# Masked attention over gathered neighbours on one core: all operations placed by a list schedule made at build time, the weighting split by slots over two engines

## The chip, the core and the metric

The kernel runs on one core of a Trainium2 chip. A core has five engines with a queue each: TensorE (PE in the profile; PEld is its weight loads) for matmuls, VectorE (DVE), ScalarE (ACT), GpSimd (POOL) and SyncE (SP), which here only issues DMAs. Engines run side by side, take their own instructions in order, and wait for each other by semaphores. Data lies in SBUF (128 partitions), in PSUM, where matmuls write, and in DRAM. The metric is the device time of one launch in microseconds, the median of several runs.

## The reference

One layer of attention on a graph of 1024 nodes, for 16 batches of 1024 x 512 inputs and 8 heads of 64. The adjacency matrix is sparse, and all batches share it:

```
h = maximum(layernorm(x), 0)
q, k, v = h @ Wq + bq, h @ Wk + bk, h @ Wv + bv        # each (16, 1024, 8 heads, 64)
scores  = einsum('bihd,bjhd->bhij', q, k) / sqrt(64) + where(adj == 0, -1e9, 0)
x       = x + einsum('bhij,bjhd->bihd', softmax(scores), v)
```

## The kernel before

The kernel never forms the 1024 x 1024 scores. It sorts the nodes by their number of neighbours (lines 124 to 155), so that a tile of 128 rows holds rows with lists of about equal length, and makes for every row the list of its neighbours (`list_of`, `longest`, `pieces`, lines 245 to 310). Tile 7 has the shortest lists, 2 entries, tile 0 the longest, 12; what the longest rows have beyond 12 goes into extra "list rows", pieces of 4 entries that stand as a tile of their own, number -1. All this is done once, and the batches begin behind it.

For each batch and each of its 8 tiles: `load_x` gathers 128 rows of x by an indirect DMA; `stats` takes mean and variance and GpSimd the power -1/2 (line 182); `norm` normalises on ScalarE; `flip` transposes on PE and copies back on ScalarE; `proj_kv` projects k and v (line 204, eight PE instructions for one projection); `store_kv` adds the bias on VectorE and stores both to DRAM through SP (lines 219 and 221).

The attention of a batch goes in 14 units (`UNITS`, lines 44 to 59), each of 2 to 4 slots of one tile's lists; 8 of the 14 have 4 slots. A slot is one neighbour for each of 128 rows. For unit i: `gather` fetches k and v rows of its slots, one indirect DMA of 512 KB for each slot, issued by GpSimd (line 348) into one of five buffers g; `multiply` (line 358) multiplies k by the queries and `score` (line 363) sums by heads, both on VectorE; ScalarE takes the exponent (line 365) and weighs v, one instruction for each slot and head (line 372). For units 10 to 12 VectorE weighs all of v instead (`BY_VECTOR`, line 378). `weigh` also folds units of 4 slots to 2 on VectorE (line 380), except in the last batch; `add_up` adds the slots in PSUM by matmuls with the identity, or for the list rows with the matrix that hands them to their owners (line 393). `finish` scales by the sum of the weights (lines 404 to 417), and GpSimd adds x (line 422) and stores the rows by an indirect DMA (line 423).

The order on PE, VectorE, ScalarE and GpSimd is written out by hand: lines 480 to 527 loop over the units. In step i stand `gather(i + 3)`, then `weigh(i - 1)`, then `multiply(i)` and `score(i)` with up to two halves of the next batch's projections between them (`HALVES`: how many in each step), then `add_up(i - 1)`, the next tile's queries and the last tile's `finish`. The projections run one batch ahead of the attention, and x is loaded three tiles ahead of them. Only SP's queue isn't ordered by hand.

Of the kernel before, what the change touches and what calls it, by code (L numbers as in the profile page):

```python
# [14 lines left out]

# [46 lines left out]
BY_VECTOR = (10, 11, 12)  # L62


def main_path(tc, x, adj, Wq, bq, Wk, bk, Wv, bv, out, sums, cover):
# [4 lines left out]
    NT = N // P  # L70
    DC = D // P
    NU = len(UNITS)
# [4 lines left out]
    with ExitStack() as ctx:  # L77
        pool = lambda name, bufs=1, **k: ctx.enter_context(tc.tile_pool(name=name, bufs=bufs, **k))
        const = pool("const")
        xpool = pool("xpool", 16)  # L80
        hpool = pool("hpool", 2)
        htpool = pool("htpool", 13)
        kvpool = pool("kvpool", 3)
        gpool = pool("gpool", 5)
        work = pool("work", 2)
        small = pool("small", 4)
        dram = pool("dram", 3, space=bass.MemoryType.DRAM)
        psum = bass.MemoryType.PSUM
        ps_h = pool("ps_h", 1, space=psum)
        ps_kv = pool("ps_kv", 2, space=psum)  # L90
        ps_q = pool("ps_q", 2, space=psum)
        ps_a = pool("ps_a", 2, space=psum)
# [65 lines left out]
        X, HN, HT, KV, ST = {}, {}, {}, {}, {}  # L158
# [4 lines left out]

        def nth(b, t):
            return b * NT + NT - 1 - t
# [8 lines left out]
        def stats(n):  # L174
            b, t = tile_at(n)
            st = small.tile([P, nc.vector.BN_STATS_DIM], F32, tag="st", name=f"st_{b}_{t}")
            mv = small.tile([P, nc.vector.BN_AGGR_DIM], F32, tag="mv", name=f"mv_{b}_{t}")
            rstd = small.tile([P, 1], F32, tag="rstd", name=f"rstd_{b}_{t}")
            nc.vector.bn_stats(st, X[n])  # L179
            nc.vector.bn_aggr(mv, st)  # L180
            nc.vector.tensor_scalar_add(rstd, mv[:, 1:2], EPS)  # L181
            nc.gpsimd.tensor_tensor(rstd, rstd, minus_half, ALU.pow)  # L182
            ST[n] = mv, rstd

        def norm(n):
            b, t = tile_at(n)
            mv, rstd = ST.pop(n)
            shift = small.tile([P, 1], F32, tag="shift", name=f"shift_{b}_{t}")
            nc.vector.scalar_tensor_tensor(shift, mv[:, 0:1], -1.0, rstd, op0=ALU.mult, op1=ALU.mult)  # L189
            HN[n] = hpool.tile([P, D], F32, tag="h", name=f"h_{b}_{t}")  # L190
            nc.scalar.activation(HN[n], X[n], AF.Relu, bias=shift, scale=rstd)  # L191

        def flip(n):
            b, t = tile_at(n)
            hn = HN.pop(n)
            pt = ps_h.tile([P, DC, P], F32, tag="pht", name=f"pht_{b}_{t}")
            for c in range(DC):
                nc.tensor.transpose(pt[:, c, :], hn[:, ts(c, P)], ident)  # L198
            HT[n] = htpool.tile([P, DC, P], F32, tag="hT", name=f"hT_{b}_{t}")
            nc.scalar.copy(HT[n], pt)  # L200
# [4 lines left out]

        KVT, PT = {}, {}
# [6 lines left out]
        def store_kv(n, j):  # L213
# [3 lines left out]
            if j == 0:  # L217
                KVT[n] = kvpool.tile([P, 2, D], F32, tag="kvt", name=f"kvt_{b}_{t}")
            nc.vector.tensor_tensor(KVT[n][:, j, :], PT.pop((n, j)), bias["kv"[j]], ALU.add)  # L219
            if j == 1:  # L220
                nc.sync.dma_start(KV[b][ts(t, P), :], KVT.pop(n).rearrange("p j d -> p (j d)"))
# [44 lines left out]
        def pieces():  # L266
# [3 lines left out]
            flag = small.tile([P, PIECES], F32, tag="flag", name="flag")  # L270
            count = small.tile([P, 1], F32, tag="count", name="count")
# [7 lines left out]
            end = small.tile([P, 1], F32, tag="end", name="end")  # L279
# [10 lines left out]
            part = small.tile([P, 1], F32, tag="part", name="part")  # L290
            nc.vector.tensor_tensor(part, place[:, 0:1], p_list[:, width - 1 : width], ALU.subtract)
            pick = small.tile([P, PIECES], F32, tag="pick", name="pick")
            nc.vector.tensor_scalar(pick, iota[:, :PIECES], part, None, op0=ALU.is_equal)
            picked = small.tile([P, PIECES, PIECE], F32, tag="picked", name="picked")
# [9 lines left out]
            at = small.tile([P, SLOTS], F32, tag="at", name="at")  # L304
# [3 lines left out]
            used = small.tile([P, SLOTS], F32, tag="used", name="used")  # L308
# [4 lines left out]
        Q, PQ, G, ACC = {}, {}, {}, {}  # L313
# [3 lines left out]
        tiles = B * NT  # L317
        total = B * NU

# [9 lines left out]
        def queries(b, t):  # L329
            pt = PQ[b, t] = ps_q.tile([P, D], F32, tag="q", name=f"pq_{b}_{t}")  # L330
            if t >= 0:
                project(pt, "q", nth(b, t))
                HT.pop(nth(b, t))
            else:
                nc.tensor.matmul(pt, owner, Q[b, 0], start=True, stop=True)

        def add_bias(b, t):
            pt = Q[b, t] = PQ.pop((b, t))
            if t == 0:
                Q[b, t] = work.tile([P, D], F32, tag="q0", name=f"q0_{b}")  # L340
            if t >= 0:
                nc.vector.tensor_tensor(Q[b, t], pt, bias["q"], ALU.add)

        def gather(i):
            b, t, w, c, count = unit(i)
            G[i] = gpool.tile([P, UMAX, 2, D], F32, tag="g", name=f"g_{b}_{i % NU}")
            for s in range(count):
                nc.gpsimd.indirect_dma_start(  # L348
                    out=G[i][:, s].rearrange("p j d -> p (j d)"),
                    out_offset=None,  # L350
                    in_=KV[b][:],
                    in_offset=on(ap=index[:, c + s : c + s + 1], axis=0),
                )
# [6 lines left out]
        def score(i):  # L360
# [4 lines left out]
            nc.scalar.activation(weights[:, w, :], sc, AF.Exp, scale=HD**-0.5)  # L365
# [350 lines left out]
```

## Time and profile before

| | |
|---|---|
| time, median of 3 runs (lowest to highest) | 2898.34 us (2897.23 to 2902.49) |
| the profiled execution's own time | 2899.34 us |
| its span, first to last instruction | 2897.6 us |
| mean granted TensorE clock | 0.874 |
| mean rate over the span | 190 GB/s |
| first gather issued / first multiply | 156.2 / 163.6 us |

The page gives for each engine the busy time and its share of the span. A group of instructions is named by line, engine, operation and tiles, `out<-in`, followed by its count, its busy time and mean length, and by the idle time of its engine just before such instructions with what ended it. The view of waits sums those idle times by who waited for whom. The timeline gives start and length in us from the start of the span. Lengths within a queue can overlap a little, since an instruction starts while the one before it writes its last results.

### The profile page before, as it was taken

How to read it: one execution, taken by the hardware profiler on the slowest of the kernel's cores; microseconds unless marked ns; L12 is line 12 of the kernel's file. 1: busy time of each engine (PE TensorE's matmuls, PEld its weight loads, DVE VectorE, ACT ScalarE, POOL GpSimd, SP SyncE). 2: the span in 40 equal slices, each digit the busy share in tenths (PEclk: the TensorE clock that was granted, in tenths of full speed). 3: DMA queues.
4: the chain of work that ended last, by engine and by line, in shares of the span. 5: the costliest groups of instructions: out<-in, count | busy, mean ns of one | idle time of the engine just before them, and what ended most of it. 6: DMA issues, size and time to landing. Idle time of an engine off the chain costs nothing.

```text
span 2897.6 us, 20683 instructions
## 1 busy us (share of the span) xinstructions
PE 2125.6 (73%) x4727; PEld 915.5 (32%) x4727; DVE 1772.4 (61%) x2426; ACT 1339.5 (46%) x5142; POOL 1345.2 (46%) x1298
## 2 busy tenths in 40 slices
PE   3777776877867777776867777687777867777675
PEld 1333332333323333332323333233333323333221
DVE  6744664657566575665747566474755647566675
ACT  1143364453635535364453535535363453535573
POOL 2144444454545455444544444544544445454552
PEclk9898898988988888888988988888888988988897
DMA  5155546565555556556565655556555555555673
GB/s 196 62 200 170 194 169 213 180 215 186 196 178 196 198 196 208 191 167 218 188 215 178 210 171 188 208 195 211 188 181 197 189 207 184 204 178 181 237 242 117
DMA packets 153953, 550.66 MB, mean 190 GB/s; under 512 B 18784, under 2 KB 18784, under 8 KB 153824
## 3 DMA queue, kind: packets, MB, share of 16 engines
q0 software_dynamic: 132224, 474.02, 48.4%
q1 hardware_dynamic: 21600, 75.24, 6.6%
q8 instruction: 41, 0.67, 0.1%
q14 instruction: 88, 0.72, 0.1%
HBM read 448.53 MB, written 100.66 MB: 190 GB/s over the span
## 4 chain that ended last, share of the span: by engine, by line
DVE 22%; issue 22%; ACT 21%; POOL 17%; DMA 11%; PE 7%; POOLq 0%; DVEq 0%; SPq 0%; ACTq 0%
ACT g L372 20%; POOL g L348 11%; DMA x<-in_x_dram,perm 10%; DVE scores L363 7%; DVE g L358 3%; PE acc L393 3%; DVE g L380 3%; DVE kvt L219 2%; POOL o L422 2%; DVE st L179 2%; POOL out_dram L423 2%; PE pv L204 2%; PE pk L204 1%; DMA g<-kv,index 1%; DVE g L378 1%
## 5 line engine op out<-in xcount | busy, mean ns | idle before, releaser
L372 ACT ACTIVATE g<-g,weights 128x64 f32<-128x64 f32 x4608 | 1119.9, 333 | 11.4 <-issue 3.6
L348 POOL DMA_INDIRECT g<-kv,index x768 | 776.5, 1011 | 415.7 <-issue 218.7
L393 PE MATMUL acc<-g,ident 128*128 128x512 f32 x988 | 574.9, 711 | 391.1 <-DVE g L380 245.8
L365 ACT ACTIVATE weights<-scores 128x32 f32<-128x32 f32 (+2 forms) x224 | 43.0, 192 | 1138.2 <-DVE scores L364 1129.7
L204 PE MATMUL pk<-wk,hT 128*128 128x512 f32 x1024 | 529.5, 666 | 0.0
L422 POOL TENSOR_TENSOR o<-o,x 128x512 f32<-128x512 f32 x128 | 164.3, 1284 | 708.3 <-DVE o L417 707.0
L204 PE MATMUL pq<-wq,hT 128*128 128x512 f32 x1024 | 473.6, 606 | 0.0
L204 PE MATMUL pv<-wv,hT 128*128 128x512 f32 x1024 | 468.8, 601 | 0.0
L380 DVE TENSOR_TENSOR g<-g 128x1024 f32<-128x1024 f32 x120 | 147.0, 1225 | 496.9 <-ACT g L372 495.4
L363 DVE TENSOR_REDUCE scores<-g 128x32 f32<-128x2048 f32 (+2 forms) x224 | 444.0, 1982 | 5.9 <-ACT weights L365 2.8
L393 PEld LDWEIGHTS acc<-g,ident 128*128 128x128 f32 x988 | 204.2, 219 | 701.6 <-issue 326.5
L198 PE MATMUL pht<-ident,h 128*128 128x128 f32 x512 | 101.3, 330 | 326.2 <-ACT h L191 319.9
L179 DVE BATCH_NORM_STATS2 st<-x 128x6 f32<-128x512 f32 x128 | 88.3, 690 | 345.9 <-DMA x<-in_x_dram,perm 313.4
L358 DVE TENSOR_TENSOR g<-g,pq 128x2048 f32<-128x2048 f32 (+2 forms) x160 | 296.9, 1856 | 4.7 <-DMA g<-kv,index 4.0
L204 PEld LDWEIGHTS pk<-wk,hT 128*128 128x128 f32 x1024 | 214.3, 221 | 227.5 <-issue 227.5
L204 PEld LDWEIGHTS pq<-wq,hT 128*128 128x128 f32 x1024 | 202.1, 198 | 260.6 <-issue 259.6
L204 PEld LDWEIGHTS pv<-wv,hT 128*128 128x128 f32 x1024 | 199.7, 195 | 256.9 <-issue 254.0
L182 POOL TENSOR_TENSOR rstd<-rstd,minus_half 128x1 f32<-128x1 f32 x128 | 132.3, 1034 | 303.9 <-DVE rstd L181 297.6
L191 ACT ACTIVATE h<-x,shift,rstd 128x512 f32<-128x512 f32 x128 | 103.8, 811 | 290.6 <-DVE shift L189 279.7
L198 PEld LDWEIGHTS pht<-ident,h 128*128 128x128 f32 x512 | 65.0, 163 | 435.2 <-ACT h L191 426.5
L170 POOL DMA_INDIRECT x<-in_x_dram,perm x128 | 129.9, 1015 | 71.5 <-DVE perm L155 39.3
L423 POOL DMA_INDIRECT out_dram<-o,perm x128 | 132.3, 1033 | 36.3 <-POOL o L422 33.5
(138 smaller groups left out, 1090.6 us busy)
## 6 DMA issues: line engine op xcount, KB each, us to landing
kv<-kvt SPq DMA_DIRECT2D x128, 512.0 KB, 2.6
g<-kv,index POOLq DMA_INDIRECT x768
adj<-in_adj_dram SPq DMA_DIRECT2D x8, 512.0 KB, 8.0
x<-in_x_dram,perm POOLq DMA_INDIRECT x128
out_dram<-o,perm POOLq DMA_INDIRECT x128
wk<-in_L_gnn_Wk_dram SPq DMA_DIRECT2D x1, 1024.0 KB
wv<-in_L_gnn_Wv_dram SPq DMA_DIRECT2D x1, 1024.0 KB
wq<-in_L_gnn_Wq_dram SPq DMA_DIRECT2D x1, 1024.0 KB
```

The source lines that it names most:

```text
L179: nc.vector.bn_stats(st, X[n])
L182: nc.gpsimd.tensor_tensor(rstd, rstd, minus_half, ALU.pow)
L198: nc.tensor.transpose(pt[:, c, :], hn[:, ts(c, P)], ident)
L204: nc.tensor.matmul(pt, HT[n][:, c, :], W[name][:, c, :], start=(c == 0), stop=(c == DC - 1))
L348: nc.gpsimd.indirect_dma_start(out=G[i][:, s].rearrange("p j d -> p (j d)"), out_offset=None, in_=KV[b][:], in_offset=on(ap=index[:, c + s ...
L358: nc.vector.tensor_tensor(k, k, Q[b, t][:, None, :].to_broadcast([P, count, D]), ALU.mult)
L363: nc.vector.tensor_reduce(sc, heads(G[i][:, :count, 0, :]), AX.X, ALU.add)
L372: nc.scalar.activation(v[:, s, h, :], v[:, s, h, :], AF.Identity, scale=weights[:, c + s, h : h + 1])
L380: nc.vector.tensor_tensor(v[:, 0:2], v[:, 0:2], v[:, 2:4], ALU.add)
L393: nc.tensor.matmul(ACC[b, home], owner_t if t < 0 else ident, v[:, s, :], start=(u == units[0] and s == 0), stop=(u == units[-1] and s == ...
L422: nc.gpsimd.tensor_tensor(o, o, X.pop(nth(b, t)), ALU.add)
L423: nc.gpsimd.indirect_dma_start(out=out_rows, out_offset=on(ap=perm[:, t : t + 1], axis=0), in_=o[:], in_offset=None, element_offset=b * N * D)
```

## The change

A planner (`Plan`, `plan_of`) replaces the order written out by hand. It lists every operation with its engine, a length, a place (the unit in which it is wanted), what it comes after and which buffers it uses. It then walks through time: an engine that is free takes the operation with the lowest place that has all it needs and a buffer. The order in which operations were taken is the order in which they are written, so each engine's queue is fixed when the program is built.

Four things change in the work itself. The last slot of every unit (`BY_VECTOR = {2: 1, 3: 1, 4: 1}`) is weighted by VectorE, with an exponent of its own, and the others by ScalarE; before, VectorE did all slots of units 10 to 12 and none of the others. A unit of 4 slots is folded twice, to 2 and to 1, so that PE adds one slot for it. The power -1/2, its variance and its shift are taken for pairs of tiles. And the queries of tile 0 stay in PSUM, with a copy by ScalarE for the list rows' query. Pools for small tiles are larger (8 instead of 4); the number of big buffers is the same.

```diff
-BY_VECTOR = (10, 11, 12)
+BY_VECTOR = {2: 1, 3: 1, 4: 1}
+POOLS = dict(x=16, h=2, pht=1, hT=13, pkv=2, kvt=3, q=2, q0=1, g=5, acc=2, o=2)
+class Plan:
+    def add(self, key, engine, length, place, after=(), uses=(), delay=0.15, moves=0.0):
+        self.number[key] = len(self.ops)
+        self.ops.append((key, engine, length, place, after, uses, delay, moves))
+    def ordered(self, bufs):
...
+        while True:
+            for e in engines:
+                if free[e] > now:
+                    continue
+                passed = []
+                while ready[e]:
+                    place, i = heapq.heappop(ready[e])
+                    key, _, length, _, _, uses, delay, moves = ops[i]
+                    if can_start(ops[i]):
...
+                        result.append(key)
+                        free[e] = end = now + length
...
+def plan_of(B):
...
+    for n in range(tiles):
+        b, j = divmod(n, NT)
+        p = (b - 1) * NU + j * rate
+        add(("load_x", n), "POOL", 1.25, p - 7, uses=[("x", n)], delay=4.5, moves=0.75)
+        add(("stats", n), "DVE", 0.9, p - 5, [("load_x", n)], [("x", n)])
+        if n % 2:
+            add(("variance", n // 2), "DVE", 0.16, p - 5, [("stats", n - 1), ("stats", n)])
+            add(("power", n // 2), "POOL", 0.6, p - 4.4, [("variance", n // 2)])
+            add(("shift", n // 2), "DVE", 0.16, p - 4.4, [("power", n // 2)])
...
+        for s, slot in enumerate(slots):
+            add(slot, "POOL", 1.25, i - 4 + 0.1 * s, stored, [g], delay=4.0, moves=1.5)
+        vector = BY_VECTOR[count]
+        add(("multiply", i), "DVE", 0.15 + 0.533 * count, i, slots + [q_of[q]], [g, q])
+        add(("score", i), "DVE", 0.35 + 0.533 * count, i + 0.01, [("multiply", i)], [g])
+        add(("exponent", i), "ACT", 0.4, i + 0.1, [("score", i)])
+        weighed = [("weigh_v", i)]
+        add(("weigh_v", i), "DVE", 0.15 + 0.533 * vector, i + 0.6, [("exponent", i)], [g])
+        for s in range(count - vector):
+            weighed.append(("weigh_s", i, s))
+            add(("weigh_s", i, s), "ACT", 1.97, i + 0.5 + 0.1 * s, [("exponent", i)], [g])
+        if folds(b, B, count):
+            add(("fold", i, 2), "DVE", 1.22, i + 1.3, weighed, [g])
+            add(("fold", i, 1), "DVE", 0.69, i + 1.35, [("fold", i, 2)], [g])
+            weighed = [("fold", i, 1)]
...
+def folds(b, B, count):
+    return count == 4 and b < B - 1
...
+        def exponent(i):
+            b, t, w, c, count = unit(i)
+            nc.scalar.activation(weights[:, w, :], scores[:, w, :], AF.Exp, scale=HD**-0.5)
+            own = scores[:, c + count - BY_VECTOR[count] : c + count, :]
+            nc.scalar.activation(own, own, AF.Exp, scale=HD**-0.5)
+        def weigh_v(i):
+            b, t, w, c, count = unit(i)
+            n = BY_VECTOR[count]
+            v = heads(G[i][:, count - n : count, 1, :])
+            own = scores[:, c + count - n : c + count, :, None]
+            nc.vector.tensor_tensor(v, v, own.to_broadcast([P, n, H, HD]), ALU.mult)
+        def fold(i, n):
+            v = G[i][:, :, 1, :]
+            nc.vector.tensor_tensor(v[:, 0:n], v[:, 0:n], v[:, n : 2 * n], ALU.add)
...
-            count = 2 if count == 4 and b < B - 1 else count
+            count = 1 if folds(b, B, count) else count
...
-        for n in range(min(3, tiles)):
-            load_x(n)
-        with tc.manual_schedule(engines={mybir.EngineType.PE, mybir.EngineType.DVE, mybir.EngineType.Activation, mybir.EngineType.Pool}):
...
+        with tc.manual_schedule(engines=set(engines)):
+            for name, *args in plan_of(B):
+                do[name](*args)
```

Three places show the order. In the rows a tile's name is followed by batch and unit (`g_8_9` is the buffer of batch 8, unit 9) or by batch and tile (`pk_9_1`), and then by the number of its buffer. First VectorE in batch 8, before, from the reduction of unit 9 to the multiply of unit 10:

```order
L363 TENSOR_REDUCE scores_205<-g_8_9_7923 128x32
L364 TENSOR_TENSOR scores_205<-scores_205,mask_201 128x32
L342 TENSOR_TENSOR q0_8_8184<-pq_8_0_8141,bq_rows_135 128x512
L404 TENSOR_REDUCE sums_58<-weights_206 128x8
L413 TENSOR_SCALAR sums_58<-sums_58 128x8
L415 RECIPROCAL inv_8_2_8188<-sums_58 128x8
L417 TENSOR_TENSOR o_8_2_8190<-acc_8_2_8003,inv_8_2_8188 128x512
L380 TENSOR_TENSOR g_8_9_7923<-g_8_9_7923 128x2x512
L179 BN_STATS st_10_5_8200<-x_10_5_8127 128x6
L180 BN_AGGR mv_10_5_8201<-st_10_5_8200 128x2
L181 TENSOR_SCALAR rstd_10_5_8202<-mv_10_5_8201 128x1
L358 TENSOR_TENSOR g_8_10_7971<-g_8_10_7971,q0_8_8184 128x4x512
```

And in the changed kernel, from the mask of unit 10 to its first fold:

```order
L551 TENSOR_TENSOR scores_211<-scores_211,mask_207 128x32
L574 TENSOR_TENSOR g_8_9_7690<-g_8_9_7690 128x2x512
L405 TENSOR_TENSOR kvt_9_1_7938<-pk_9_1_7913,bk_rows_133 128x512
L574 TENSOR_TENSOR g_8_9_7690<-g_8_9_7690 128x512
L564 TENSOR_TENSOR g_8_10_7785<-g_8_10_7785,scores_211 128x512
L545 TENSOR_TENSOR g_8_11_7811<-g_8_11_7811,pq_8_-1_7908 128x4x512
L372 SCALAR_TENSOR_TENSOR shift_40_7969<-mv_40_7740,rstd_40_7775 128x2
L405 TENSOR_TENSOR kvt_9_1_7938<-pv_9_1_7940,bv_rows_137 128x512
L550 TENSOR_REDUCE scores_211<-g_8_11_7811 128x32
L551 TENSOR_TENSOR scores_211<-scores_211,mask_207 128x32
L615 TENSOR_TENSOR o_8_1_7988<-acc_8_1_7936,inv_8_1_7888 128x512
L574 TENSOR_TENSOR g_8_10_7785<-g_8_10_7785 128x2x512
```

Before, a unit's fold (L380) stood between its own reduction and the next unit's multiply. Now the fold of unit 9 (L574, `128x2x512`) stands behind the reduction of unit 10, and that of unit 10 behind the reduction of unit 11; the second fold (`128x512`) follows one instruction later, and the weighting of the last slot (L564) stands behind the previous unit's folds.

Second PE at the same place of the program. Before, from the queries of tile 0 to the accumulation of unit 10:

```order
L204 MATMUL pq_8_0_8141<-wq_133,hT_8_0_7135 128x512 x4
L393 MATMUL acc_8_1_8146<-g_8_8_7880,ident_111 128x512 x2
L198 MATMUL pht_10_6_8207<-ident_111,h_10_6_8139 128x128 x4
L204 MATMUL pk_10_7_8214<-wk_125,hT_10_7_8074 128x512 x4
L204 MATMUL pv_10_7_8225<-wv_129,hT_10_7_8074 128x512 x4
L393 MATMUL acc_8_1_8146<-g_8_9_7923,ident_111 128x512 x2
L335 MATMUL pq_8_-1_8242<-q0_8_8184,owner_202 128x512
L198 MATMUL pht_10_5_8256<-ident_111,h_10_5_8238 128x128 x4
L204 MATMUL pk_10_6_8263<-wk_125,hT_10_6_8212 128x512 x4
L204 MATMUL pv_10_6_8273<-wv_129,hT_10_6_8212 128x512 x4
L393 MATMUL acc_8_0_8288<-g_8_10_7971,ident_111 128x512 x2
```

And now:

```order
L394 MATMUL pq_8_0_7851<-wq_139,hT_8_0_7062 128x512 x4
L589 MATMUL acc_8_2_7781<-g_8_7_7573,ident_117 128x512 x3
L385 MATMUL pht_9_0_7901<-ident_117,h_9_0_7787 128x128 x4
L522 MATMUL pq_8_-1_7908<-q0_8_7891,owner_208 128x512
L394 MATMUL pk_9_1_7913<-wk_131,hT_9_1_7805 128x512 x4
L589 MATMUL acc_8_1_7936<-g_8_8_7661,ident_117 128x512
L394 MATMUL pv_9_1_7940<-wv_135,hT_9_1_7805 128x512 x4
L589 MATMUL acc_8_1_7936<-g_8_9_7690,ident_117 128x512
L394 MATMUL pk_9_0_7975<-wk_131,hT_9_0_7918 128x512 x4
L385 MATMUL pht_10_7_8002<-ident_117,h_10_7_7981 128x128 x4
L394 MATMUL pv_9_0_8009<-wv_135,hT_9_0_7918 128x512 x4
L589 MATMUL acc_8_0_8038<-g_8_10_7785,ident_117 128x512
```

A unit of 4 slots takes one matmul of the accumulation (the rows of `acc`) instead of two, and the projections of the next batch stand one at a time between the accumulations.

Third GpSimd, from the gather of unit 8 on. Before:

```order
L348 DMA g_8_8_7880<-kv_8_6514,index_200 128x1024 x4
L422 TENSOR_TENSOR o_8_4_7919<-o_8_4_7919,x_8_4_6517 128x512
L423 DMA out_0_dram<-o_8_4_7919,perm_141 16384x512
L348 DMA g_8_9_7923<-kv_8_6514,index_200 128x1024 x4
L170 DMA x_10_7_7928<-in_x_dram,perm_141 128x512
L348 DMA g_8_10_7971<-kv_8_6514,index_200 128x1024 x4
L182 TENSOR_TENSOR rstd_10_7_7978<-rstd_10_7_7978,minus_half_116 128x1
L422 TENSOR_TENSOR o_8_3_8039<-o_8_3_8039,x_8_3_6565 128x512
L423 DMA out_0_dram<-o_8_3_8039,perm_141 16384x512
L348 DMA g_8_11_8043<-kv_8_6514,index_200 128x1024 x4
L170 DMA x_10_6_8048<-in_x_dram,perm_141 128x512
L182 TENSOR_TENSOR rstd_10_6_8064<-rstd_10_6_8064,minus_half_116 128x1
```

And now:

```order
L535 DMA g_8_8_7661<-kv_8_6473,index_206 128x1024 x4
L535 DMA g_8_9_7690<-kv_8_6473,index_206 128x1024 x4
L622 TENSOR_TENSOR o_8_4_7663<-o_8_4_7663,x_8_4_6081 128x512
L625 DMA out_0_dram<-o_8_4_7663,perm_147 16384x512
L368 TENSOR_TENSOR rstd_39_7736<-rstd_39_7736,minus_half_122 128x2
L351 DMA x_10_4_7753<-in_x_dram,perm_147 128x512
L368 TENSOR_TENSOR rstd_40_7775<-rstd_40_7775,minus_half_122 128x2
L535 DMA g_8_10_7785<-kv_8_6473,index_206 128x1024 x4
L535 DMA g_8_11_7811<-kv_8_6473,index_206 128x1024 x4
L622 TENSOR_TENSOR o_8_3_7790<-o_8_3_7790,x_8_3_6198 128x512
L625 DMA out_0_dram<-o_8_3_7790,perm_147 16384x512
L351 DMA x_10_3_7870<-in_x_dram,perm_147 128x512
```

Now two units are gathered in a row, and two powers for pairs of tiles (L368) stand almost together; before, a residual (L422), a load of x or a power stood between any two gathers. Loads of x stand further ahead: that of tile 3 of batch 10 is in these rows, ahead of the gather of unit 12 of batch 8, where before tile 6 stood (tiles go from 7 down to 0).

More of the change, by code (lines that the diff above doesn't have):

```diff
@@ L16 @@
+import heapq
 from contextlib import ExitStack
@@ L69, in main_path @@
     B, N, D = x.shape
-    NT = N // P
     DC = D // P
-    NU = len(UNITS)
+    assert N == NT * P
     x_rows = x.rearrange("b n d -> (b n) d")
@@ L278, in pieces @@
             nc.vector.tensor_copy(begin, before)
-            end = small.tile([P, 1], F32, tag="end", name="end")
+            end = once.tile([P, 1], F32, tag="end", name="end")
             nc.vector.tensor_tensor(end, begin, count, ALU.add)
```

397 lines of the change are left out of this document (212 added, 185 removed).

## The prediction

> **What bounds the kernel now.** I read the profile's page first: shares of the engines, chain, DMA queues.
>
> ```profile
> span 2897.6 us, 20683 instructions
> PE 2125.6 (73%) x4727; PEld 915.5 (32%) x4727; DVE 1772.4 (61%) x2426; ACT 1339.5 (46%) x5142; POOL 1345.2 (46%) x1298
> ...
> q0 software_dynamic: 132224, 474.02, 48.4%
> q1 hardware_dynamic: 21600, 75.24, 6.6%
> ...
> DVE 22%; issue 22%; ACT 21%; POOL 17%; DMA 11%; PE 7%; POOLq 0%; DVEq 0%; SPq 0%; ACTq 0%
> ACT g L372 20%; POOL g L348 11%; DMA x<-in_x_dram,perm 10%; DVE scores L363 7%; DVE g L358 3%; PE acc L393 3%; DVE g L380 3%; DVE kvt L219 2%; POOL o L422 2%; DVE st L179 2%; POOL out_dram L423 2%; PE pv L204 2%; PE pk L204 1%; DMA g<-kv,index 1%; DVE g L378 1%
> ```
>
> No engine is full: the busiest, PE, at 73%, the transfers at 48.4 + 6.6 = 55% of the 16 DMA engines. The chain runs through all of them in turn. So the order makes the time, and the view of waits says where (columns: total us, times, longest).
>
> ```profile
> DVE g L380 <- ACT g L372: 495.4, 75, 7.6
> DVE st L179 <- DMA x<-in_x_dram,perm: 313.4, 50, 12.3
> DVE kvt L219 <- PE pv L204: 97.6, 45, 3.5
> DVE kvt L219 <- PE pk L204: 44.4, 16, 8.5
> ...
> DVE pq L342 <- PE pq L204: 25.9, 28, 3.1
> DVE sums L411 <- PE p_more L410: 21.6, 16, 9.6
> ...
> DVE o L417 <- issue: 0.2, 1, 0.2
> ```
>
> VectorE waits 495 us for ScalarE's weighting and 313 us for x. The 26 rows of this view, from the first to the last shown, add up to 1076 us of its 2897.6 - 1772.4 = 1125 us of idle time; the other 50 us are gaps between instructions. One such wait in the timeline (start, length, instruction, idle time before it and its releaser):
>
> ```profile
> 1403.59 1.88 PE L393 MATMUL acc<-g,ident 128*128 128x512 f32 x4
> 1403.61 2.28 DVE L363 TENSOR_REDUCE scores<-g 128x32 f32<-128x2048 f32 x1
> ...
> 1406.45 7.74 ACT L372 ACTIVATE g<-g,weights 128x64 f32<-128x64 f32 x32
> ...
> 1414.22 1.23 DVE L380 TENSOR_TENSOR g<-g 128x1024 f32<-128x1024 f32 x1 [7.50 <-ACT g L372]
> ...
> 1415.50 3.45 PE L393 MATMUL acc<-g,ident 128*128 128x512 f32 x4 [6.61 <-DVE g L380]
> ...
> 1419.22 0.94 POOL L348 DMA_INDIRECT g<-kv,index  x1 [8.76 <-PE acc L393]
> ```
>
> The fold stands in VectorE's queue ahead of the next unit's multiply, so VectorE stands still for the 7.74 us that ScalarE weighs. PE stands still behind the fold, and the gathers behind PE. PE then needs 3.45 us for what took 1.88 us at 1403.59: after the pause it runs at about half speed.
>
> **The change part by part, from VectorE's side.** By my count VectorE has the most left to do afterwards, so the sum is made on it.
>
> ```profile
> L372 ACT ACTIVATE g<-g,weights 128x64 f32<-128x64 f32 x4608 | 1119.9, 333 | 11.4 <-issue 3.6 <-ACT weights L365 1.5
> L393 PE MATMUL acc<-g,ident 128*128 128x512 f32 x988 | 574.9, 711 | 391.1 <-DVE g L380 245.8 <-issue 108.2 <-ACT g L372 29.8
> L380 DVE TENSOR_TENSOR g<-g 128x1024 f32<-128x1024 f32 x120 | 147.0, 1225 | 496.9 <-ACT g L372 495.4
> L378 DVE TENSOR_TENSOR g<-g,scores 128x2048 f32<-128x2048 f32 x48 | 109.5, 2280 | 4.1 <-ACT scores L367 4.1
> L417 DVE TENSOR_TENSOR o<-acc,inv 128x512 f32<-128x512 f32 x128 | 88.5, 692 | 7.5 <-issue 0.2
> L181 DVE TENSOR_SCALAR rstd<-mv 128x1 f32<-128x1 f32 x128 | 19.7, 154 | 5.0
> L189 DVE SCALAR_TENSOR_TENSOR shift<-mv,rstd 128x1 f32<-128x1 f32 x128 | 19.3, 150 | 4.2 <-POOL rstd L182 4.2
> L367 ACT ACTIVATE scores<-scores 128x32 f32<-128x32 f32 x48 | 9.2, 192 | 0.0
> ```
>
> *Weighting by slots.* Each of the 224 units gets one 128x512 multiplication on VectorE; at the 692 ns of L417 (same shape) that is 155 us, for the 109.5 us of L378: +45 us. ScalarE weighs 544 slots instead of 576: 32 x 8 x 0.243 us (1119.9/4608) = -62 us. It gains 176 small exponents at no more than 0.19 us, +33 us. ScalarE goes to about 1310 us and is hidden.
>
> *Folds to one slot.* 120 more folds of 128x512 at 0.69 us: +83 us on VectorE. PE loses 240 instructions of 0.47 us (1.88/4), about 113 us.
>
> *Pairs.* 64 each of L181 and L189 go: -19 us. GpSimd loses 64 powers.
>
> So VectorE has +45 + 83 - 19 = **+109 us** of work.
>
> *Order.* This is what must pay. In the new order the fold of unit 9 stands behind the multiply and reduction of unit 10. Between the reduction of unit 10 and its own fold stand ten instructions of other work, by the rows above (1.23 + five of 0.69 + two of about 2.28 + 0.35) some 9.6 us. ScalarE needs 24 x 0.243 + 0.4 = 6.2 us for three slots. So the 495 us are covered, with about 3 us to spare; if a copy and two norms fall in between, the cover is just gone. Loads of x are issued as soon as a buffer is free, a pair of statistics ahead, so I put the 313 us at nothing; the cover is a lead of about one batch.
>
> A new wait comes in: VectorE's share of the weighting waits for two exponents on ScalarE, which stand behind the previous unit's weighting, and evictions, row sums and the next multiply stand behind it. L378 waited so before, 4.1 us in 48; for 224 that is 19 us. For tile 0 a copy on ScalarE instead of VectorE's write feeds the list rows' query. Both go into the stall term below. SP's queue still holds the same 128 stores in the same tile order; nothing is moved past it.
>
> The waits for PE (97.6 + 44.4 + 25.9 + 21.6 = 190 us) have no such reason to vanish, because PE gets nearly as full as VectorE:
>
> ```profile
> 1400.15 3.60 PE L204 MATMUL pq<-wq,hT 128*128 128x512 f32 x8
> ...
> L198 PE MATMUL pht<-ident,h 128*128 128x128 f32 x512 | 101.3, 330 | 326.2 <-ACT h L191 319.9
> ```
>
> 384 projections x 3.60 = 1382, 816 accumulations x 0.47 = 384, transposes 101, some 25 for the rest: at most 1892 us at the fast rate. VectorE has 1772 + 109 + 50 = 1931 us. Two engines so close, each waiting for the other in a fixed order, don't overlap perfectly: a batch's first half has 5 of the 8 query projections and most unfolded slots and is PE's, its second half has six four-slot units and is VectorE's. The stall term lies between nothing and all of today's 190 us (plus half of the x waits, 157, if the lead isn't kept); I take half of the 190: **95 us**.
>
> The sum goes by stages:
>
> ```profile
> 0.00:163.60 163.60, 91.25 (x210) 41.67 (x211) 104.78 (x197) 17.77 (x26) 34.01 (x44) 0.92 0.37 129
> 163.60:2870.00 2706.40, 2026.86 (x4506) 871.35 (x4504) 1663.17 (x2216) 1314.34 (x5086) 1308.80 (x1251) 0.87 0.57 196
> 2870.00:2897.60 27.60, 7.48 (x12) 2.48 (x12) 4.45 (x14) 7.40 (x32) 2.35 (x3) 0.61 0.04 12
> ```
>
> The columns are length, then busy us of PE, weight loads, VectorE, ScalarE and GpSimd; clock, DMA share, GB/s. The first cut is at the first multiply (timeline), and the row below it is from the view of waits between 45 and 163.6 us:
>
> ```profile
> 163.60 1.22 DVE L358 TENSOR_TENSOR g<-g,pq 128x1024 f32<-128x1024 f32 x1 [3.96 <-DMA g<-kv,index]
> ...
> DVE kvt L219 <- PE pk L204: 26.0, 8, 4.1
> ```
>
> The new order lays the list work evenly between the projections, which should cover about half of these 26 us, so I take 150 for 163.6 (bounds 140 and 164). The main part is VectorE's 1663 + 109 + 50 = 1822. The tail is 27.6 with 32 weightings at its head, now 24: 25.5. Without stalls 150 + 1822 + 25.5 = 1998; with 95 it is 2093 us of span. The profiled execution took 2899.34 us for its span of 2897.6, 1 us from the median of 2898.34; so +1.7, and rounded **2095 us**.
>
> One rule speaks against the folds.
>
> ```profile
> L182 POOL TENSOR_TENSOR rstd<-rstd,minus_half x128: 556/569/2660, 46.5 to 2673.3; 128x1 f32<-128x1 f32 x128
> ...
> 1400.80 2.29 DVE L358 TENSOR_TENSOR g<-g,q 128x2048 f32<-128x2048 f32 x1
> ...
> 1400.87 2.65 POOL L182 TENSOR_TENSOR rstd<-rstd,minus_half 128x1 f32<-128x1 f32 x1
> ...
> L422 POOL TENSOR_TENSOR o<-o,x 128x512 f32<-128x512 f32 x128 | 164.3, 1284 | 708.3 <-DVE o L417 707.0 <-issue 0.9
> ```
>
> A power takes 569 ns at the median, and 2.65 us when a multiply with both inputs in SBUF has just begun. The Trainium skill, "SBUF — State Buffer", section "Who interferes with whom", says that a VectorE instruction with two SBUF inputs and a GpSimd one that reads SBUF exclude each other, the later waiting for the whole earlier one. This trace agrees (2.65 is 0.57 behind the rest of 2.29). By that rule the 240 folds would now and then meet a residual or a power (164 + 64 x 0.57 = 200 us of 2095, 10%) and lose half of 1.28 us: an estimate of 15 us more, 2110. The forecast doesn't contain it.
>
> **Rivals.**
>
> *PE becomes the bound.* For it: the 3.45 us row, half speed after a pause, and PE's pauses would now fall in each batch's second half. Against it: with fewer pauses there is less slow time. PE's busy time before was 2125.6, with its slow stretches; less 113 it is 2013, and the pauses at both ends (163.6 - 91.3 and 20) stay: 2105; with half of VectorE's former 190 us of coupling 2200 us. The Trainium skill, "TensorE: Matmul & The Clock Gate", section "What's actually happening", gives half rate after an idle window of about 3.4 us; by it this rival holds if pauses of that length come in most batches.
>
> *The five g buffers become the bound.* A gather waits for the accumulation five units back:
>
> ```profile
> POOL g L348 <- PE acc L393: 171.8, 35, 11.2
> POOL o L422 <- DVE o L417: 707.0, 109, 23.6
> ```
>
> The DMA work, 55% of 2898 = 1594 us, would be 76% of 2095, so landings come later. If the 171.8 us pass through to VectorE whole, on top of 2095: 2270 us.
>
> *The change doesn't do what it says.* The fold waits stay because ScalarE is late behind copies and norms: half of 495 on top of 2095, 2340 us. Against it stands the 9.6 against 6.2 us.
>
> *Slower.* GpSimd keeps its order too: a residual waits for VectorE's scaling with gathers queued behind it (the 707 us row, 6.5 us each, hidden today behind gathers already landed). If no gather is ahead any more, VectorE waits for the gather, and the 128 residuals pay in turn. It takes (2898 - 1998)/128 = 7.0 us at each to be slower than now; with the 6.5 us and one issue of 0.94 us it is 1998 + 128 x 7.44 = 2950.
>
> **How the numbers follow.** Forecast (1998 to 2150) 0.60; PE bound 0.18; g buffers 0.12; fold waits stay 0.06; slower 0.04. The range leaves out the slower case and whatever drifts further than these bounds: its low end is the sum without stalls, with a first multiply at 140 and 10 us fewer gaps, 1980; its high end adds all of the 190 and half of the x waits to 1998: 2345. A measurement of this kernel can tell about 0.2% from no change. Faster by more has 0.95, same 0.01, slower 0.04.
>
> **What would show it.** Right: the wait of the fold for ScalarE below 100 us; VectorE at 1880 us of work and about 90% of the span; PE's granted clock above 0.91 in the middle; statistics no longer waiting for x; the first multiply near 150. Wrong: VectorE waiting for gathers (g buffers), long waits for pk, pv and pq at a low clock (PE), or residual waits followed at once by gathers that VectorE waits for (slower). The prediction falls if the fixed order drifts, so that small delays on one engine pass to all of them.

## The result, and the profile after

| | before | changed |
|---|---|---|
| time, median (lowest to highest) | 2898.35 us (2897.23 to 2902.49) | 2056.62 us (2049.97 to 2062.7) |
| ratio, 95% interval | 1 | 0.7094 (0.7069 to 0.7118) |
| span of the profiled execution | 2897.6 us | 2048.2 us |
| mean granted TensorE clock | 0.874 | 0.970 |

The forecast was 2095 us, 1.9% above the time. The first page of the changed kernel's profile:

```profile
span 2048.2 us, 19935 instructions
PE 1827.0 (89%) x4487; PEld 812.4 (40%) x4487; DVE 1848.6 (90%) x2594; ACT 1291.4 (63%) x5078; POOL 1260.5 (62%) x1234
...
q0 software_dynamic: 132224, 474.02, 66.6%
q1 hardware_dynamic: 21600, 75.24, 9.5%
```

VectorE went from 61% to 90% and PE from 73% to 89%. The busy time hardly changed on VectorE (1772.4 to 1848.6); what went is idle time, 1125 us of it down to 2048.2 - 1848.6 = 199.6. The view of waits of the changed kernel says which (total us, times, longest):

```profile
DVE sums L607 <- PE p_more L606: 28.9, 13, 3.9
DVE shift L372 <- POOL rstd L368: 18.2, 12, 3.2
DVE g L564 <- ACT scores L557: 15.2, 6, 7.1
DVE kvt L405 <- PE pk L394: 15.0, 9, 4.4
DVE kvt L405 <- remote: 12.1, 3, 4.1
DVE kvt L405 <- PE pq L394: 9.1, 3, 4.2
```

The fold's wait for ScalarE, 495.4 us before, and that of the statistics for x, 313.4 us, are no longer among the largest rows ("remote" is a releaser that the trace doesn't name). The rows of the groups, with the idle time just before each behind the second bar, show the fold and the new weighting:

```profile
L564 DVE TENSOR_TENSOR g<-g,scores 128x512 f32<-128x512 f32 x224 | 151.9, 678 | 21.6 <-ACT scores L557 15.2 <-ACT weights L555 5.7 <-issue 0.6
L574 DVE TENSOR_TENSOR g<-g 128x1024 f32<-128x1024 f32 x120 | 151.1, 1260 | 1.0 <-ACT weights L555 1.0
L574 DVE TENSOR_TENSOR g<-g 128x512 f32<-128x512 f32 x120 | 92.5, 771 | 0.0
```

The same kind of place in the timeline as in the prediction, one unit's weighting and its fold:

```profile
1399.28 5.83 ACT L570 ACTIVATE g<-g,weights 128x64 f32<-128x64 f32 x24
1401.07 0.68 DVE L405 TENSOR_TENSOR kvt<-pk,bk_rows 128x512 f32<-128x512 f32 x1
1401.67 0.68 DVE L564 TENSOR_TENSOR g<-g,scores 128x512 f32<-128x512 f32 x1
1402.38 2.30 DVE L550 TENSOR_REDUCE scores<-g 128x32 f32<-128x2048 f32 x1
1404.71 0.20 DVE L551 TENSOR_TENSOR scores<-scores,mask 128x32 f32<-128x32 f32 x1
1404.82 0.68 DVE L405 TENSOR_TENSOR kvt<-pv,bv_rows 128x512 f32<-128x512 f32 x1
...
1406.03 1.22 DVE L574 TENSOR_TENSOR g<-g 128x1024 f32<-128x1024 f32 x1 [0.53 <-ACT weights L555]
```

While ScalarE weighs for 5.83 us, VectorE evicts, weighs another slot and reduces the next unit; the fold comes when ScalarE is done. Last the stages, cut at the first multiply (144.30) and at the start of the last weighting (2023.09); the columns are those of the prediction:

```profile
0.00:144.30 144.30, 92.77 (x246) 43.94 (x247) 109.40 (x208) 20.35 (x31) 41.47 (x49) 0.99 0.46 161
144.30:2023.09 1878.79, 1727.83 (x4227) 766.13 (x4226) 1733.81 (x2372) 1265.19 (x5024) 1216.67 (x1183) 0.97 0.80 281
2023.09:2048.20 25.11, 6.40 (x16) 2.31 (x16) 5.39 (x16) 5.84 (x25) 2.33 (x3) 0.74 0.04 13
```

### The profile page after: what moved, and what is told of

It is laid out like the page before. It is cut to its first block, busy times and chain, and to the rows that moved or that the text cites. A ratio compares the mean times of both kernels' runs of the same rounds, so it can differ in the third digit from the quotient of the medians.

```text
span 2048.2 us, 19935 instructions
## 1 busy us (share of the span) xinstructions
PE 1827.0 (89%) x4487; PEld 812.4 (40%) x4487; DVE 1848.6 (90%) x2594; ACT 1291.4 (63%) x5078; POOL 1260.5 (62%) x1234
## 5 line engine op out<-in xcount | busy, mean ns | idle before, releaser
L570 ACT ACTIVATE g<-g,weights 128x64 f32<-128x64 f32 x4352 | 1067.3, 336 | 5.8 <-issue 5.4
L394 PE MATMUL pk<-wk,hT 128*128 128x512 f32 x1024 | 488.4, 622 | 8.0 <-ACT hT L390 7.4
L589 PE MATMUL acc<-g,ident 128*128 128x512 f32 x778 | 380.5, 612 | 34.7 <-DVE g L574 19.4
L545 DVE TENSOR_TENSOR g<-g,pq 128x2048 f32<-128x2048 f32 (+2 forms) x208 | 405.5, 1953 | 0.8 <-DMA g<-kv,index 0.3
L394 PEld LDWEIGHTS pk<-wk,hT 128*128 128x128 f32 x1024 | 202.0, 201 | 254.9 <-issue 242.6
L574 DVE TENSOR_TENSOR g<-g 128x1024 f32<-128x1024 f32 x240 | 243.7, 1015 | 1.0 <-ACT weights L555 1.0
L589 PEld LDWEIGHTS acc<-g,ident 128*128 128x128 f32 x778 | 144.7, 193 | 215.9 <-issue 167.2
L622 POOL TENSOR_TENSOR o<-o,x 128x512 f32<-128x512 f32 x128 | 167.5, 1309 | 30.6 <-DVE o L615 27.4
L564 DVE TENSOR_TENSOR g<-g,scores 128x512 f32<-128x512 f32 x224 | 151.9, 678 | 21.6 <-ACT scores L557 15.2
L385 PE MATMUL pht<-ident,h 128*128 128x128 f32 x512 | 83.5, 288 | 65.4 <-ACT h L378 48.1
L405 DVE TENSOR_TENSOR kvt<-pk,bk_rows 128x512 f32<-128x512 f32 x128 | 87.3, 682 | 39.8 <-PE pk L394 15.0
```

Source lines behind the costliest of these rows:

```text
L385: nc.tensor.transpose(PH[n][:, c, :], hn[:, ts(c, P)], ident)
L394: nc.tensor.matmul(pt, HT[n][:, c, :], W[name][:, c, :], start=(c == 0), stop=(c == DC - 1))
L545: nc.vector.tensor_tensor(k, k, Q[b, t][:, None, :].to_broadcast([P, count, D]), ALU.mult)
L564: nc.vector.tensor_tensor(v, v, own.to_broadcast([P, n, H, HD]), ALU.mult)
L570: nc.scalar.activation(v[:, h, :], v[:, h, :], AF.Identity, scale=weights[:, c + s, h : h + 1])
L574: nc.vector.tensor_tensor(v[:, 0:n], v[:, 0:n], v[:, n : 2 * n], ALU.add)
```

## Experiments

Two questions were open behind a forecast that came close. Did the order pay, as the prediction has it, or the work that changed with it? And is what is left set by VectorE's work, by PE, or by the buffers? Each ratio is against the kernel before on the same chip (2893.07 to 2898.89 us).

### Order alone and work alone

The changed kernel's planner with the work of before (VectorE weighs units 10 to 12 whole, folds end at two slots; the pairs, the larger pools for small tiles and the queries of tile 0 in PSUM stay):

```diff
-BY_VECTOR = {2: 1, 3: 1, 4: 1}
+def by_vector(u, count):
+    return count if u in (10, 11, 12) else 0
...
-        vector = BY_VECTOR[count]
+        vector = by_vector(u, count)
...
-            add(("fold", i, 1), "DVE", 0.69, i + 1.35, [("fold", i, 2)], [g])
-            weighed = [("fold", i, 1)]
+            weighed = [("fold", i, 2)]
```

> The planner's order with the weighting and folds of before: VectorE weighs all slots of units 10 to 12, ScalarE all others, folds go to two slots; power by pairs stays. Theory A: near the changed kernel; VectorE has about 100 us less, PE 110 us more than in the changed kernel, so PE bounds it: 2100 to 2200 us. Theory B: 2600 us or more.

Measured: 2038.83 us, ratio 0.704 (0.7023 to 0.7056), faster than expected and than the changed kernel. And the order of before with the new work (last slot on VectorE, folds to one slot, powers still for each tile):

```diff
+            own = scores[:, c + count - 1 : c + count, :]
+            nc.scalar.activation(own, own, AF.Exp, scale=HD**-0.5)
...
+            nc.vector.tensor_tensor(last, last, own.to_broadcast([P, 1, H, HD]), ALU.mult)
             if count == 4 and b < B - 1:
                 nc.vector.tensor_tensor(v[:, 0:2], v[:, 0:2], v[:, 2:4], ALU.add)
+                nc.vector.tensor_tensor(v[:, 0:1], v[:, 0:1], v[:, 1:2], ALU.add)
```

> The order by hand with the new weighting (last slot of each unit on VectorE) and folds to one slot. Theory A: the fold waits for 5.8 instead of 7.7 us of weighting, so the waits shrink by a quarter to a third and VectorE's work grows by about 100 us: 2650 to 2850 us. Theory B: below 2350 us.

Measured: 2992.77 us, ratio 1.0332 (1.0307 to 1.0357). This kernel's rows by groups, VectorE:

```profile
L377 DVE TENSOR_TENSOR g<-g,scores 128x512 f32<-128x512 f32 x224 | 152.3, 680 | 10.9 <-ACT scores L366 10.9
L379 DVE TENSOR_TENSOR g<-g 128x1024 f32<-128x1024 f32 x120 | 147.5, 1229 | 507.2 <-ACT g L370 507.1
L380 DVE TENSOR_TENSOR g<-g 128x512 f32<-128x512 f32 x120 | 83.0, 692 | 4.1
```

So the new order has the whole gain without the new weighting and folds, and these alone make the kernel slower. No run takes the larger pools and the queries in PSUM apart from the order; but a kernel that has them too, with another order (the one planned with false lengths, below), takes 2569.59 us. ScalarE's weighting got shorter by a slot, and yet the fold waits 507 us, where it had waited 495: the stall passed from a long wait in some units (75 times, up to 7.6 us) to a shorter one in nearly all (119 times, up to 5.1 us). VectorE's busy time rose by 116 us (1772.4 to 1888.5) and the span by 96: in this order added work stands in line with the waits. The expectation of a faster kernel was wrong.

### One wait at a time in the order of before

First a unit's weighting and fold, with its accumulation behind them, moved behind the next unit's reduction:

```diff
-                if i:
-                    weigh(i - 1)
...
-                if i:
-                    add_up(i - 1)
                 if len(todo) < 2:
                     score(i)
+                if i:
+                    weigh(i - 1)
+                    add_up(i - 1)
```

> The kernel before with one move: weighing and folding of unit i-1 stand behind the reduction of unit i instead of ahead of its multiply. Theory A (order: VectorE standing behind the fold is the first cost): most of the 495 us of waits for ScalarE goes, part comes back as waits for PE and x; 2450 to 2650 us. Theory B (the division of the work between engines made the gain): no less than 2800 us.

Measured: 2817.91 us, ratio 0.9736 (0.971 to 0.9762). Its view of waits:

```profile
DVE st L179 <- DMA x<-in_x_dram,perm: 455.8, 77, 12.0
DVE kvt L219 <- PE pk L204: 197.2, 55, 9.2
DVE pq L342 <- PE pq L204: 108.5, 51, 4.6
DVE kvt L219 <- PE pv L204: 106.4, 79, 3.1
DVE g L380 <- ACT g L372: 44.2, 31, 2.2
```

The fold's wait fell by 451 us, but the wait for x rose by 142, that for pk by 153 and that for pq by 83. Of 451 us the span got 80. Theory A had the mechanism, and its range was far too low, since nearly all of the wait came back elsewhere; the time lies in the range of theory B. Then, on top of it, the loads of x ahead of the step's gather in GpSimd's queue:

```diff
-                if n + 3 < tiles:
+                if n + 3 < tiles and h < 2 * NT:
                     before.append((load_x, n + 3))
...
+                for h in todo:
+                    if h % 2 and h // 2 + 3 < tiles:
+                        load_x(h // 2 + 3)
                 if i + 3 < total:
                     gather(i + 3)
```

> The kernel with the later fold (2818 us) and one more move: in each step the loads of x stand ahead of the gather of unit i+3 in GpSimd's queue, where that gather waits for PE. Theory A (one wait hides behind another in the hand order: x was late because its load stood behind a gather that waits for the accumulation): the 456 us of waits for x fall below 200, the time goes to 2500 to 2650 us. Theory C (PE's half-speed stretches and waits for PE's projections take the place): 2700 us or more.

Measured: 2600.92 us, ratio 0.8982 (0.8961 to 0.9004). Its view of waits:

```profile
DVE kvt L219 <- PE pk L204: 221.3, 91, 10.0
DVE kvt L219 <- PE pv L204: 176.4, 121, 3.1
DVE pq L342 <- PE pq L204: 122.9, 76, 4.5
DVE st L179 <- DMA x<-in_x_dram,perm: 55.1, 25, 4.6
```

Now PE is waited for, 520 us in these three rows (34 us in the rows of the changed kernel that name PE ahead of the same instructions). The two moves by hand bring 294 us (2894.69 to 2600.92) of the 842 of the change; the rest needs PE's projections, too, to stand where nobody waits for them, which is what a schedule of all engines together does.

### Does the schedule need its lengths?

The changed kernel, planned as if every operation took 1.0:

```diff
-        self.ops.append((key, engine, length, place, after, uses, delay, moves))
+        self.ops.append((key, engine, 1.0, place, after, uses, delay, moves))
```

> The changed kernel with every length in the planner set to 1.0 us (landing delays and transfer times as they were): another order from the same places. If the planner needs true lengths: 2150 us or more, with waits of VectorE for ScalarE and for PE. If the places alone make the order: within 1.5% of 2057 us.

Measured: 2569.59 us, ratio 0.8878 (0.8858 to 0.8898). VectorE's idle time is 686 us (span 2569.3, busy 1883.0). With every length at 1.0 the places and the rest of the change bring 11%, and the lengths the rest of the gain.

### What is left: the second fold, the small units, the buffers, the pairs

The changed kernel with folds to two slots only:

```diff
-            add(("fold", i, 1), "DVE", 0.69, i + 1.35, [("fold", i, 2)], [g])
-            weighed = [("fold", i, 1)]
+            weighed = [("fold", i, 2)]
```

> The changed kernel with units folded to two slots only, planned anew: PE gets 240 instructions more, VectorE 120 folds fewer. If PE and VectorE bound it together: VectorE's relief is worth nothing and PE's 110 us show for the most part, 2090 to 2160 us. If VectorE alone bounds it: 83 us less, 1970 to 2000 us.

Measured: 1984.58 us, ratio 0.6856 (0.684 to 0.6871), 72 us less than the changed kernel. VectorE's busy time falls by 78 us to 1770.9, and the time is in the range of the theory of VectorE alone: the trade of VectorE's work for PE's was a loss. But PE, 94% busy over the span (1868.9 us), has nothing left to give here. The columns are those of the stages; the first row is the changed kernel, the second this one:

```profile
144.30:1900.00 1755.70, 1632.75 (x4035) 729.48 (x4034) 1626.27 (x2248) 1176.43 (x4647) 1141.19 (x1111) 0.98 0.80 282
144.30:1900.00 1755.70, 1729.83 (x4387) 787.74 (x4385) 1606.28 (x2198) 1220.22 (x4827) 1175.69 (x1147) 1.00 0.82 291
```

PE goes from 93.0% to 98.5% of this stretch, VectorE from 92.6% to 91.5%. So PE has become the bound, and what VectorE's 78 us are worth by themselves isn't known from this run. Next, units of 2 and 3 slots weighed by ScalarE alone:

```diff
-BY_VECTOR = {2: 1, 3: 1, 4: 1}
+def by_vector(u, count):
+    return 1 if count == 4 else 0
```

> The changed kernel with the units of 2 and 3 slots weighed by ScalarE alone: VectorE has 96 multiplications of 0.68 us less (65 us), ScalarE 186 us more. If VectorE's work alone sets the time of the changed kernel: 1985 to 2005 us. If VectorE, PE and ScalarE set it together, or the longer ScalarE chain shows: 2040 us or more.

Measured: 1955.32 us, ratio 0.6757 (0.6742 to 0.6772). That is below the range of the theory. It is 101 us less for 24 us less busy time on VectorE (1824.6); the idle time fell by 71 us. The 96 weightings did take 65 us with them, but the folds and two kinds of small instructions, unchanged in number, took 44 us longer (the last section shows what can hold them up). Both edits together:

> Folds to two slots (1985 us) and units of 2 and 3 slots weighed by ScalarE alone: VectorE at about 1705 us of work, PE at 1869. If VectorE still set the time: about 1925 us. If PE, 94% busy in the kernel with folds to two, is the bound there: no gain, 1970 to 1995 us.

Measured: 1984.79 us, ratio 0.6857 (0.6841 to 0.6872). That is the time of the kernel with folds to two slots (1984.58), with 52 us less on VectorE (1719.3 us) and VectorE's idle time up at 265. PE is again 98.5% busy behind the start:

```profile
150.00:1900.00 1750.00, 1724.12 (x4360) 785.39 (x4359) 1547.20 (x2093) 1370.06 (x5439) 1180.68 (x1139) 1.00 0.82 290
```

So PE is the bound in both kernels, and a better division may lie between: units 12 and 13 folded to two slots, the other six to one, and small units by ScalarE alone.

```diff
+def left(u):
+    return 2 if u >= 12 else 1
...
-            add(("fold", i, 1), "DVE", 0.69, i + 1.35, [("fold", i, 2)], [g])
-            weighed = [("fold", i, 1)]
+            weighed = [("fold", i, 2)]
+            if left(u) == 1:
+                add(("fold", i, 1), "DVE", 0.69, i + 1.35, weighed, [g])
+                weighed = [("fold", i, 1)]
```

> The changed kernel with units of 2 and 3 slots weighed by ScalarE alone, and units 12 and 13 folded only to two slots, the other six units of 4 slots to one. Against the kernel with small units by ScalarE alone (1955.3): VectorE loses 30 folds of 0.70 to 0.85 us = 21 to 25 us, PE gains 30 accumulations of 0.45 us = 13 us. Theory A (VectorE alone decides up to where PE is about 94% busy): 1928 to 1945. Theory B (both are so full that the coupling eats it): 1950 to 1965.

Measured: **1920.2 us**, ratio 0.6633 (0.6616 to 0.6649), 6.6% below the changed kernel, below both expectations, and the fastest of all. Its page:

```profile
span 1918.7 us, 20616 instructions
PE 1805.8 (94%) x4547; PEld 811.1 (42%) x4547; DVE 1779.6 (93%) x2468; ACT 1458.6 (76%) x5750; POOL 1259.0 (66%) x1234
```

Both engines are now at 93 to 94% of the span (PE at 97.5% and VectorE at 95.0% between 150 and 1900 us). Four buffers g instead of five in the changed kernel (`POOLS`, `g=4`):

> The changed kernel with four buffers g instead of five. Theory A (the buffers are not near the bound; VectorE's work decides): within 2050 to 2090. Theory B (the prediction's rival: five buffers are just enough, a gather waits for the accumulation five units back): with four, VectorE waits for gathers in most units, and the time is 2150 or more, with a row of multiply (DVE g) waiting for DMA of over 80 us.

Measured: 2054.0 us, ratio 0.7088 (0.7067 to 0.711), no change; VectorE waits 12.7 us for gathers. And powers for each tile instead of pairs:

```diff
-        if n % 2:
-            add(("variance", n // 2), "DVE", 0.16, p - 5, [("stats", n - 1), ("stats", n)])
+        add(("variance", n), "DVE", 0.16, p - 5, [("stats", n)])
...
-        add(("norm", n), "ACT", 0.81, p - 3.8, [("shift", n // 2)], [("x", n), ("h", n)])
+        add(("norm", n), "ACT", 0.81, p - 3.8, [("shift", n)], [("x", n), ("h", n)])
```

> The changed kernel, with variance, power and shift for every tile again instead of pairs of tiles. Both theories have 128 more small VectorE instructions here, 64 x (0.154 + 0.150) = 19 us. Theory A (the pairs save what the prediction said): VectorE gains 19 us of work and the time rises to 2065 to 2085. Theory B (the 128x2 variance is held up by GpSimd, as its longest of 1.73 us against 0.155 us for 128x1 before suggests, and a pair waits for its later tile): what the pairs save is given back, and the time is 2045 to 2062; the 128x1 variance then shows no length above 0.2 us.

Measured: 2000.33 us, ratio 0.6912 (0.6895 to 0.6929). It is 56 us faster with 26 us more busy time on VectorE (1875.1), which neither theory had. Two were formed: pairs cost by themselves, or the order happened to fit better. The same edit in the fastest kernel tells them apart:

> The kernel with small units by ScalarE alone and units 12 and 13 folded only to two slots (1920.2), with variance, power and shift for every tile again instead of pairs of tiles. Theory A (pairs cost by themselves, since two tiles come free at once and bunch the norms on ScalarE and the transposes on PE; undoing them took 56 us off the changed kernel): 1870 to 1905. Theory B (undoing pairs helped the changed kernel only because its fixed order happened to drift less, while VectorE's waits for ScalarE and PE are already small here, 6.3 + 16 us): VectorE gets 64 x 0.30 = 19 us more work, and the time is 1915 to 1940.

Measured: 1952.16 us, ratio 0.6741 (0.673 to 0.6752), 32 us slower and beyond even theory B, so nothing here shows that pairs cost by themselves. The planner decides everything anew after any edit: with and without pairs VectorE has 1701 operations in common (all but variance and shift), and only 543 of them are followed by the same one in both orders; for four buffers it is 667, for the small units 583 of 1605. VectorE's idle time for the nine full schedules lies anywhere between 121 us (each tile's own power) and 271 us (work of before). The same edit gave 56 us in one order and cost 32 us in another, so the price of an edit under the planner is known only to some 50 us. The 72 us of the second fold are near its 78 us of work, but with PE nearly full that may be chance; how much of the 101 us for the small units is theirs stays open, and so does what in an order makes it fit.

## Why the prediction was right, by its steps

*The sum.* The mechanism (order takes away the waits for ScalarE and for x) and the time were right; one term was mis-sized, VectorE's work, and another, the idle time, came out right by luck. The step was "VectorE has +45 + 83 - 19 = **+109 us** of work". By the stages:

| stage | predicted | measured |
|---|---|---|
| to the first multiply | 150 | 144.3 |
| main part, VectorE's work | 1663 + 109 = 1772 | 1733.8 |
| main part, idle | 50 + 95 = 145 | 1878.8 - 1733.8 = 145.0 |
| tail | 25.5 | 25.1 |

Nearly the whole miss, 38 of 45 us, is that work. By rows it is more than priced: weighting 151.9 - 109.5 = +42 (for +45), second folds +92.5 (for +83), the first folds +4, pairs 14.4 + 16.0 - 39.0 = -9 (for -19): +130. But rows overlap. VectorE's groups add up to 1863.0 us before, 91 more than the busy 1772.4, and to 1993.4 after, 145 more than 1848.6. In the timeline above an instruction of 0.68 us is followed 0.60 us later by the next; ahead of a wait nothing follows, and nothing is saved. In the trace of before 1111 of VectorE's instructions overlap with the next one, after 1772, each by 0.083 us at the median. So the overlaps grew by 54 us, and +130 became +76. The Trainium skill, "Perfetto Trace Analysis", section "Optimizing Scalar/DVE Operations", says that a profiled instruction's second half of access overhead, the acknowledgement of its writes, overlaps with the next instruction, with some 60 ns on SBUF for VectorE; the traces agree with the overlap, at 83 ns.

*Order.* The fold's wait went from 495 to 1.0 us, that for x from 313 to 4.8. The new order with the old weighting and folds gave 0.704.

*Stalls.* That the main part's idle time is 145 us, as forecast, is luck. It was to be 50 us of gaps and 95 of waits. The view of waits between 144.3 and 2023.09 us adds up to 122 us, and the gaps are the other 23. Of the 122 us the rows that name PE have 53 and those of an unnamed releaser 17.5; 18.7 are for the two exponents (priced at 19), and 21.6 stand ahead of `shift`, which needs GpSimd's power of a pair of tiles. That last wait was 4.2 us before, and the sum had no term for it.

Half of the waits for PE was to stay "because PE gets nearly as full as VectorE". PE did get as full (1727.8 us of the main part, VectorE 1733.8). Over the nine full schedules the idle time is 210 to 271 us in the three where PE has 1868.9 us of work or more, and 121 to 200 where it has 1787.4 to 1835.1. Among these six it doesn't follow PE's work (121 us at 1816.2, 200 at 1827.0); how well the fixed order fits may make that difference, but no run shows it.

*PE as the bound.* Not in the changed kernel, where neither engine is full: with 42 us more on PE and 78 less on VectorE it was faster. But the rival was only one edit away, since PE is the bound in that faster kernel. In the main part PE stood still for 151 us, where it had stood still for 680, and its granted clock there rose from 0.87 to 0.97 (over 0.91 was to show it).

*Buffers.* Ruled out: four do as well as five, and VectorE waits 0.3 us for gathers with five, 12.7 with four.

*The change doesn't do what it says; slower.* The fold wait is gone. GpSimd's wait of residuals, 707 us, is down to 27.4, and VectorE doesn't wait for gathers (0.8 us ahead of the multiplies).

*The rule against the folds.* The estimate of 15 us more came out, by luck in its parts. In the changed kernel 52 of the 240 folds overlap with an elementwise instruction of GpSimd (about 24 were expected), and each of these is about 0.30 us longer than the others at their median (0.64 was expected): 15.6 us. One reading beside it was off: the power of 2.65 us ended 0.43 us behind the multiply's end, not 0.57.

*What the prediction did not ask* is whether the new weighting and folds pay within the new order. The sum carried them as +109 us on VectorE and -113 on PE. No gain of theirs shows: 2056.62 against 2038.83 without them, a difference that a redrawn order could also make.

## What to carry to other kernels

In a kernel whose engines each wait for another through hand-ordered queues, taking one wait away mostly moves it: 451 us less at the fold were 80 us less of span. Plan all queues together, with measured lengths, and only then balance the work, by moving some units at a time between the two busiest engines. With such a planner every edit redraws the whole order, so compare busy time and idle time apart, look whether the same instructions have become longer, and don't credit an edit with an idle-time difference that another redraw would also give.

## What the runs showed of the hardware

Very small VectorE instructions can be held up by GpSimd. The views of single lines give count, shortest, median and longest ns. In the kernel before, the lower bound of the sums (128x8) and the variance (128x1) hardly vary. None of these sums began while GpSimd ran an elementwise instruction.

```profile
L413 DVE TENSOR_SCALAR sums<-sums x128: 171/172/174, 191.5 to 2879.9; 128x8 f32<-128x8 f32 x128
L181 DVE TENSOR_SCALAR rstd<-mv x128: 153/153/155, 46.2 to 2673.0; 128x1 f32<-128x1 f32 x128
```

In the changed kernel the same two, the variance now 128x2, reach 1.85 and 1.73 us:

```profile
L609 DVE TENSOR_SCALAR sums<-sums x128: 171/172/1852, 148.2 to 2025.3; 128x8 f32<-128x8 f32 x128
L365 DVE TENSOR_SCALAR rstd<-mv x64: 117/158/1733, 47.3 to 1872.3; 128x2 f32<-128x2 f32 x64
```

One such place in its timeline, first VectorE's rows, then GpSimd's:

```profile
530.90 0.64 DVE L609 TENSOR_SCALAR sums<-sums 128x8 f32<-128x8 f32 x1
531.57 0.20 DVE L611 RECIPROCAL inv<-sums 128x8 f32<-128x8 f32 x1
...
530.23 1.27 POOL L622 TENSOR_TENSOR o<-o,x 128x512 f32<-128x512 f32 x1
```

The residual ends at 531.50, and the 0.17 us instruction, started in its midst, at 531.54. All 11 sums that began within a residual took 0.41 us or more, and two of five variances did. The two longest rows began while GpSimd still issued an indirect DMA, and a residual followed it; 16 others that began in such an issue took 0.33 to 0.40 us, and most that did were not held up. For one element in each partition there is no such case. In the kernel before, 8 of the 128 variances (128x1) began within a residual, and all 8 took 0.153 or 0.154 us:

```profile
228.40 1.26 POOL L422 TENSOR_TENSOR o<-o,x 128x512 f32<-128x512 f32 x1 [5.71 <-DVE o L417]
...
229.16 0.15 DVE L181 TENSOR_SCALAR rstd<-mv 128x1 f32<-128x1 f32 x1
```

The Trainium skill, "SBUF — State Buffer", section "Who interferes with whom", says that `tensor_scalar` can enter a mode that uses both ports, and that VectorE in such a mode and GpSimd then exclude each other: the one that issues first holds the ports for its whole instruction, and the other blocks. The trace agrees for 2 and 8 elements, and shows no such case for 1.

The folds pay, too: the 29 folds of 128x512 that overlap with an elementwise instruction of GpSimd took 1047 ns in the mean and the other 91 took 683; for 128x1024 it is 1437 ns for 23 and 1218 for 97. How often the two meet depends on the order, and such a wait counts as busy time: with four buffers the variance took 739 ns in the mean, and VectorE was busy for 57 us more than with five, without a change in the time.
